# A graph-attention layer and a graph-convolution layer on one core: the last chunk's parts for Wo moved forward, and the residuals' biases added by accumulating transfers

## The chip, the cores and the metric

The kernel runs on one core of a Trainium2 chip. The metric is the device time of one execution in microseconds. Before the change it is 2554.0 us, the median of 3 runs (2552.22 to 2556.43).

## What is computed

The input `x` has 64 samples of 256 rows by 512 columns in float32; `adj` is a 256 by 256 matrix of zeros and ones. Two layers follow one another, each ending in a residual sum and a layer norm.

```python
# layer 0: attention over 8 heads of 64, masked by adj
q, k, v = x @ Wq + bq, x @ Wk + bk, x @ Wv + bv
attn = softmax(q k^T / 8 + (1 - adj) * -1e9)
x = layernorm(x + (attn @ v) @ Wo + bo)
# layer 1: graph convolution
x = layernorm(x + (adj @ x) @ weight + bias)
```

## The kernel before

The samples are worked off in 32 pairs (512 rows). Software pipelining turns each pair's work into a "window": in window `w` the kernel does the attention of pair `w`, the projections v, q, k of pair `w + 1`, and the second layer and the output product of pair `w - 1`. A window repeats 30 times; a different sequence opens and another closes the run.

The products with the five weights are made in three parts to keep float32 accuracy on a faster multiplication: every left factor is cut into `high`, `low` and `diff`, and so is every weight. VectorE makes the cuts. For the second factor of Wo (called `o`) and of the second layer's weight (`l`) the left factor is cut in four chunks of 128 rows:

```python
    def cut_low(a, cut, low):
        nc.vector.tensor_scalar(cut.bitcast(I32), a.bitcast(I32), -int(FINE), None, op0=OP.bitwise_and)
        nc.vector.tensor_tensor(low, a, cut, op=OP.subtract)
    # [...]
    def chunk_parts(name, p, j):          # one chunk: three VectorE instructions
        a = (O if name == "o" else Y)[p, j // 2][:, j % 2].rearrange("p k i -> p (k i)")
        cut = one.tile([P, D], F32, name="cut")
        high, low = (chunks.tile([P, D], F32R, name=n) for n in ("chigh", "clow"))
        diff = differences.tile([P, D], F32R, name="cdiff")
        cut_low(a, cut, low)
        difference(a, low, diff)
        # [...]
        later(1, chunk_high, name, p, j)  # ScalarE copies the high part one step later
    # [...]
    def near(name, p, j):                 # TensorE: low part first, then high
        chunk_high(name, p, j)
        pm = BANKS[name, p, j] = ps_mm.tile([P, D], F32, name="mm")
        if (name, p, 1) in WP:
            part_product(pm, name, p, j, 1)
        part_product(pm, name, p, j, 0)
        # [...]
    def far(name, p, j):                  # TensorE: the diff part, later
        # [...]
```

`later(n, f)` puts a step off by `n` ticks; a tick passes after each block of products. In the windows the orders of TensorE, ScalarE and VectorE are those in which the program names the steps. GpSimd's order is chosen by the scheduler.

The three parts of each weight lie in device memory and are loaded again for every window, in tiles of 1 MB, through a ring of six tiles, by GpSimd's DMA queue:

```python
    def load_w(n=1):
        # [...] the order is o, v, q, k, l in each window, three parts each
                t = wring.tile([P, DC, D], F32R, name="wr")
                nc.gpsimd.dma_start(t, SCRATCH[name, i])
```

The residual `R` of a pair is loaded by SyncE's queue into one of two buffers, 1 MB each, as soon as the pair that held the buffer has been stored. The biases are added to it by VectorE, one instruction of 128 x 1024 for each sample and layer:

```python
    def load_r(p):
        t = rpool.tile([P, 2, NC, D], F32, name="r")
        nc.sync.dma_start(t, xr[p])
    # [...]
    def biased(p, b, bias):
        nc.vector.tensor_tensor(R[p][b], R[p][b], bias[:, None, :].to_broadcast([P, NC, D]), op=OP.add)

    def with_bo(p, b):
        biased(p, b, bo_s)
```

`bo_s` holds `bo` plus the product of `bv` and Wo, on all partitions; `b1_s` the second layer's bias. The bias of the second layer is added when `R`'s rows have been read for `adj @ x` (`later(1, biased, p, b, b1_s)` in `adj_x`).

The attention's exponentials of a unit lie in two tiles, `e0` and `e1`. VectorE multiplies each by the mask (`masked`), then sums both (`summed`) for the denominators. The order of a window is put together here:

```python
            later(1 + kc, masked, p, u, kc)
    # [...]
        seq = slot + co[2:3] + o[:1] + f1 + co[3:] + o[1:2] + PENDING[:6] + o[2:] + PENDING[6:] + slot + v + q[:1] + slot + q[1:] + f1 + \
            y[:1] + f0 + y[1:2] + k[:1] + (cl[:1] if w < NP - 2 else []) + y[2:] + f0 + bo_steps + slot + k[1:2] + \
            (cl[1:2] if w < NP - 2 else [])
```

`slot` is an attention unit, `co`/`cl` are the cuts of the chunks of Wo and of the second layer, `o`, `v`, `q`, `k`, `l` the blocks of products, `y` the products with `adj`, `f1`/`f0` the `far` parts that are still owed (all but one, or all), `PENDING` the cuts of the next input.

Of the kernel before, what the change touches and what calls it, by code (L numbers as in the profile page):

```python
# [20 lines left out]
F32 = mybir.dt.float32  # L21
# [3 lines left out]
OP = mybir.AluOpType  # L25
AX = mybir.AxisListType

P = 128
# [9 lines left out]
def tile_adj_resnorm(tc, x, adj, wq, bq, wk, bk, wv, bv, wo, bo, w1, b1, out):  # L38
    good = fast(tc, x, adj, wq, bq, wk, bk, wv, bv, wo, bo, w1, b1, out)
    with tc.If(good < P):  # L40
        general(tc, x, adj, wq, bq, wk, bk, wv, bv, wo, bo, w1, b1, out)


def fast(tc, x, adj, wq, bq, wk, bk, wv, bv, wo, bo, w1, b1, out):

    nc = tc.nc
    B, N, D = x.shape
    HD = D // H
    DC = D // P
    NC = N // P  # L50
    NP = B // 2
# [19 lines left out]
    scratch = pool("scratch", 1, space=bass.MemoryType.DRAM)  # L71
# [8 lines left out]
    XC, R, XF, XG, XL, XD, Q, K, V, E, SM, O, HL, Y, ST, CP, CUT = ({} for _ in range(17))  # L80
# [27 lines left out]
    def on_all(b, name):  # L108
        t = cpool.tile([P, D], F32, name=name)
        nc.sync.dma_start(t, b.partition_broadcast(P))  # L110
        return t
# [18 lines left out]
    def raw_weight(name, tiles, queue):  # L130

        for i in range(3):
            SCRATCH[name, i] = scratch.tile([P, DC, D], F32, name=f"{name}{i}")
        n = DC // len(tiles)
        for i, t in enumerate(tiles):
            for k in range(n):
                RAW[name, i * n + k] = t[:, k]
            w = SOURCE[name][i * n * P:(i + 1) * n * P]
            if name == "o":


                for a in range(n):
                    queue.dma_start(t[:, a], w.rearrange("(h a i) e -> a h i e", h=4, a=2)[a])
            else:
                queue.dma_start(t, w.rearrange("(c p) e -> p c e", p=P))
# [44 lines left out]
    bo_s, b1_s = on_all(bo, "bo"), on_all(b1, "b1")  # L190
# [7 lines left out]
    def adj_t():  # L198
# [10 lines left out]
        nc.vector.tensor_reduce(acc[:, 0:1], square, AX.XY, OP.max)  # L209
        nc.vector.tensor_scalar(acc, acc, RANGE * RANGE, None, op0=OP.mult)  # L210

    def bv_wo():

        wide = one.tile([P, DC, P], F32, name="vc")
        nc.vector.tensor_copy(wide, bv_s[:, :, None].to_broadcast([P, DC, P]))
        pm = ps_mm.tile([P, D], F32, name="mm")
        for d in range(DC):
            nc.tensor.matmul(pm, wide[:, d, :], RAW["o", d], start=d == 0, stop=d == DC - 1)
        nc.vector.tensor_tensor(bo_s, bo_s, pm, op=OP.add)

# [2 lines left out]
    def later(n, f, *args):  # L225
        due.append([n, f, args])

    def tick():
        for d in due:
            d[0] -= 1  # L230
        ready = [d for d in due if d[0] <= 0]
        due[:] = [d for d in due if d[0] > 0]
        for _, f, args in ready:
            f(*args)
# [124 lines left out]
    def scores(p, u):  # L359
        g, b = UNITS[u]  # L360
        for kc in range(NC):

            sc = [ps_at.tile([P, 2, N], F32, name="at") for s in range(2)]
            for a in range(2):
                for s in range(2):
                    r = slice(s * HD, (s + 1) * HD)
                    nc.tensor.matmul(sc[s][:, a, :], K[p, g][r, a, b, kc * P:(kc + 1) * P], Q[p, g][r, a, b, :],  # L367
                                     start=True, stop=True)
            e = E[p, u, kc] = one.tile([P, 2, 2, N], F32, name=f"e{kc}")
            for s in range(2):  # L370
                nc.scalar.activation(e[:, s], sc[s], AF.Exp, scale=qscale)  # L371
            later(1 + kc, masked, p, u, kc)

    def masked(p, u, kc):
        e = E[p, u, kc].rearrange("p s a n -> p (s a) n")
# [47 lines left out]
        nc.gpsimd.tensor_tensor(acc, acc, seen, op=OP.add)  # L423


    def biased(p, b, bias):

        nc.vector.tensor_tensor(R[p][b], R[p][b], bias[:, None, :].to_broadcast([P, NC, D]), op=OP.add)

    def with_bo(p, b):  # L430
        biased(p, b, bo_s)

    def norm(p, name):

# [66 lines left out]
    def adj_x(p, i):  # L501
        b, half = divmod(i, 2)
        if half == 0:
            Y[p, b] = four.tile([P, NC, DC, P], F32, name="o")
        while (p, b, half) not in HL:
            tick()
        hl = HL.pop((p, b, half))
        pm = ps_mm.tile([P, 2, N], F32, name="mm")
        for j in range(2):
            for mc in range(NC):  # L510
                for i in range(2):
                    nc.tensor.matmul(pm[:, j, :], hl[:, i, mc, j * P:(j + 1) * P], adjT[:, mc, :],  # L512
                                     start=mc == 0 and i == 0, stop=mc == NC - 1 and i == 1)
        nc.scalar.activation(Y[p, b][:, :, 2 * half:2 * half + 2].rearrange("p c j i -> p j c i"), pm.rearrange("p j (c i) -> p j c i", c=NC), AF.Copy)
        if half:
            later(1, biased, p, b, b1_s)
        if p < NP - 2 and b == 0:
            later(1, halves, p, 1, half)

# [20 lines left out]
    def between(w):  # L540

        ahead, behind = w + 1, w - 1
        b = lambda name: [(block, name, behind if name in "ol" else ahead, j) for j in range(4)]
        v, q, k, o, l = (b(n) for n in "vqkol")
        c = lambda name, p: [(chunk_parts, name, p, j) for j in range(4)]
        y = [(adj_x, behind, i) for i in range(4)]
        bo_steps = [(with_bo, w, b) for b in range(2)]
        x_steps = [(x_t, w + 2, i) for i in range(4) if w + 2 < NP]
        x1 = [[s for f in (x_t, x_parts) for s in [(f, w + 2, i)] if w + 2 < NP] for i in range(4)]
        x2 = [[(x_diff, w + 2, i)] if w + 2 < NP else [] for i in range(4)]  # L550
        slot, f1 = [None], [(caught_up, 1)]
        f0 = [(caught_up,)]
        split = lambda name: [(split_w, name, i) for i in range(4)]
        mixed = lambda m, n: [s for pair in zip(m, n) for s in pair]
        halves_tiles = lambda: [one.tile([P, 2, D], F32, name=f"hl{i}") for i in range(2)]
        if w == -1:
            return [(x_t, 0, i) for i in range(4)] + mixed(v, split("v")) + mixed(q, split("q")) + [(adj_t,)] + \
                mixed(k, x_steps)
        if w == 0:
            raw_weight("o", halves_tiles(), nc.sync)  # L560
            PENDING[:] = [s for m, n in zip(x1, x2) for s in m + n]
            return slot + mixed(v, split("k")) + slot + q[:3] + split("o") + [(bv_wo,), (load_w, 3)] + \
                [(lambda: raw_weight("l", halves_tiles(), nc.sync),)] + slot + q[3:] + k[:2] + split("l") + \
                [(load_r, 0)] + slot + k[2:] + bo_steps + c("o", w)[:2] + \
                [(load_w, 3), (load_r, 1)]
        co, cl = c("o", behind), c("l", behind)
        seq = slot + co[2:3] + o[:1] + f1 + co[3:] + o[1:2] + PENDING[:6] + o[2:] + PENDING[6:] + slot + v + q[:1] + slot + q[1:] + f1 + \
            y[:1] + f0 + y[1:2] + k[:1] + (cl[:1] if w < NP - 2 else []) + y[2:] + f0 + bo_steps + slot + k[1:2] + \
            (cl[1:2] if w < NP - 2 else [])
        PENDING[:] = x1[3] + x2[3]  # L570
        if w == NP - 2:
            co = c("o", w)
            return seq + k[2:3] + co[:1] + k[3:] + co[1:2] + [(block, "o", w, 0)] + cl[:1] + [(block, "o", w, 1)] + cl[1:2]
        seq += k[2:3] + cl[2:3] + k[3:] + x1[0] + l[:1] + f1 + x2[0] + x1[1] + x2[1] + l[1:2] + cl[3:] + \
            l[2:3] + c("o", w)[:1] + x1[2] + x2[2] + l[3:] + f1 + c("o", w)[1:2]
        return seq

    PENDING = []

    def slot(before, unit):  # L580
        if before[0] >= 0:
            values(*before)
        scores(*unit)

    def steps(seq, units):
        for step in seq:
            if step is None:
                before = units.pop(0)
                step = slot, before, units[0]
            f, *args = step  # L590
            f(*args)
            if f in (block, slot, adj_x, values, split_w):
                tick()

    def window(w):
        steps(between(w), [(w - 1, 3)] + [(w, u) for u in range(4)])

    def last_window():
# [15 lines left out]
        def some(what):  # L614


            for word in what.split():
# [6 lines left out]
                else:  # L624
                    yield chunk_parts if word[0] == "c" else block, word[-3], pairs[word[-2]], int(word[-1])

        bo_steps = [(with_bo, q, b) for b in range(2)]
        seq = [None, (rows_of_q,), *some("lr0 cop2 lr1 cop3 op2 clr2 op3 clr3 f slot yp0 lr2 yp1"), *bo_steps,
               *some("slot coq0 lr3 coq1 oq0 clp0 oq1 clp1 f slot lp0 clp2 lp1 clp3 yq0"), (values, q, 3),
# [202 lines left out]
```

## Time and profile before

| what | value |
|---|---|
| time, median of 3 | 2554.0 us |
| span of the profiled execution | 2553.1 us |
| TensorE (PE) busy | 2496.0 us, 98% |
| VectorE (DVE) busy | 1872.6 us, 73% |
| ScalarE (ACT) busy | 1705.7 us, 67% |
| GpSimd (POOL) busy | 382.4 us, 15% |
| moved by DMA | 600.25 MB, mean 235 GB/s |
| of which GpSimd's queue (q0) | 475.03 MB, 51.9% of 16 engines' span |
| of which SyncE's queue (q1) | 121.42 MB, 22.0% of 16 engines' span |

A busy TensorE isn't a TensorE at its peak: the ends of its instructions are modelled and overlap, so what matters is the distance between the starts of neighbouring groups of products. The timeline gives these starts. A group of four products of 128 x 512 starts every 0.91 us where nothing waits. The same step of neighbouring windows starts 77.4 us apart. What VectorE does is only of interest where TensorE waits for it, and the same holds for the transfers.

### The profile page before, as it was taken

Reading aid. Unit: us, or ns where it says so; the run is one execution under the profiler, and the core shown is the slowest. Engines: PE = TensorE matmul, PEld = TensorE weight load, DVE = VectorE, ACT = ScalarE, POOL = GpSimd, SP = SyncE. Lnnn points to the kernel's source line nnn. Section 1 sums busy time; section 2 is a strip of 40 time slices with the busy share of each in tenths; the row PEclk is TensorE's granted clock in tenths of the full one; section 3 lists DMA queues with packets and bytes.
Section 4 is the critical chain, followed back from the end, with each engine's and each line's share of the span. In section 5 each row is a group of like instructions: output and inputs, shape, how many; then the busy total and the mean of one; then the engine's idle time right before and its main releaser. Section 6 shows DMA issues by size and latency. Waiting matters only on the chain.

```text
span 2553.1 us, 42184 instructions
## 1 busy us (share of the span) xinstructions
PE 2496.0 (98%) x15806; PEld 1886.6 (74%) x15806; DVE 1872.6 (73%) x3239; ACT 1705.7 (67%) x3206; POOL 382.4 (15%) x793
## 2 busy tenths in 40 slices
PE   8999999999999999999999999999999999999997
PEld 4477777777777777777777777777777777777765
DVE  4676787677886677876767876768876778866786
ACT  4557666776666766666776667766667766677755
POOL 0111111111111111111111111111111111111101
PEclk9999999999999999999999999999999999999998
DMA  7868778778788687777787787787787787777711
GB/s 205 284 201 273 235 232 259 240 244 243 240 256 247 236 263 232 235 250 252 231 274 226 232 259 243 240 262 234 246 246 247 251 247 233 247 254 229 257 68 51
DMA packets 375744, 600.25 MB, mean 235 GB/s; under 512 B 273520, under 2 KB 273776, under 8 KB 317552
## 3 DMA queue, kind: packets, MB, share of 16 engines
q0 software_dynamic: 65232, 475.03, 51.9%
q1 hardware_dynamic: 309760, 121.42, 22.0%
q8 instruction: 127, 2.08, 0.3%
q10 hardware_dynamic: 544, 1.05, 0.1%
q14 instruction: 81, 0.66, 0.1%
HBM read 548.15 MB, written 49.28 MB: 234 GB/s over the span
## 4 chain that ended last, share of the span: by engine, by line
PE 70%; DVE 25%; issue 3%; DMA 1%; ACT 0%; POOL 0%; SPq 0%; DVEq 0%; ACTq 0%
PE mm L314 50%; PE at L367 7%; PE at L402 6%; PE mm L512 5%; DVE clow L169 4%; DVE r L338 3%; DVE cdiff L174 3%; DVE diff L174 2%; DVE cut L168 2%; PE at L394 2%; DVE e L376 2%; DVE low L169 2%; DVE xT L264 2%; DVE x L168 1%; DVE o L418 1%
## 5 line engine op out<-in xcount | busy, mean ns | idle before, releaser
L326 ACT ACTIVATE mm<-mm 128x512 f32<-128x512 f32 x616 | 357.8, 581 | 356.7 <-PE mm L314 356.6
L376 DVE TENSOR_TENSOR e<-e,adjT 128x1024 f32<-128x1024 f32 x256 | 307.6, 1221 | 34.2 <-ACT e L371 34.2
L314 PE MATMUL mm<-wr,clow 128*128 128x512 f32 x1024 | 285.1, 401 | 25.1 <-DVE clow L169 24.6
L371 ACT ACTIVATE e<-at 128x512 f32<-128x512 f32 x512 | 265.2, 604 | 52.9 <-PE at L367 52.9
L314 PE MATMUL mm<-wr,chigh 128*128 128x512 f32 x1024 | 279.9, 396 | 0.7
L314 PE MATMUL mm<-wr,cdiff 128*128 128x512 f32 x1024 | 269.6, 391 | 5.9 <-ACT mm L326 5.9
L314 PE MATMUL mm<-low,wr 128*128 128x512 f32 x960 | 265.1, 398 | 0.0
L314 PE MATMUL mm<-high,wr 128*128 128x512 f32 x960 | 257.2, 390 | 0.0
L367 PE MATMUL at<-qT,kT 64*128 64x256 f32 x2048 | 256.6, 389 | 0.1
L314 PEld LDWEIGHTS mm<-wr,clow 128*128 128x128 f32 x1024 | 188.7, 190 | 86.6 <-DVE clow L169 38.3
L314 PE MATMUL mm<-diff,wr 128*128 128x512 f32 x960 | 248.5, 391 | 0.0
L402 PE MATMUL at<-e,v 128*32 128x256 f32 x4096 | 246.9, 381 | 0.0
L367 PEld LDWEIGHTS at<-qT,kT 64*128 64x128 f32 x2048 | 190.6, 186 | 67.7 <-issue 53.0
L499 DVE TENSOR_TENSOR hl<-r,hl 128x512 fp32r<-128x512 f32 x122 | 84.3, 691 | 203.4 <-ACT hl L498 203.4
L314 PEld LDWEIGHTS mm<-wr,chigh 128*128 128x128 f32 x1024 | 191.5, 189 | 53.0 <-ACT chigh L298 14.2
L314 PEld LDWEIGHTS mm<-wr,cdiff 128*128 128x128 f32 x1024 | 192.5, 188 | 48.1 <-ACT mm L326 7.8
L444 ACT ACTIVATE z<-r,mean 128x512 bf16<-128x512 f32 x240 | 172.6, 719 | 76.2 <-DVE mean L436 71.2
L314 PEld LDWEIGHTS mm<-low,wr 128*128 128x128 f32 x960 | 173.6, 188 | 51.6 <-issue 19.9
L338 DVE SCALAR_TENSOR_TENSOR r<-mm,r 128x512 f32<-128x512 f32 x240 | 160.4, 687 | 69.6 <-PE mm L314 69.6
L314 PEld LDWEIGHTS mm<-high,wr 128*128 128x128 f32 x960 | 180.3, 188 | 38.4
L476 ACT ACTIVATE r<-r,less,rstd 128x512 f32<-128x512 f32 x248 | 200.4, 808 | 6.1 <-DVE less L469 6.1
L314 PEld LDWEIGHTS mm<-diff,wr 128*128 128x128 f32 x960 | 176.3, 188 | 33.6
(123 smaller groups left out, 3985.0 us busy)
## 6 DMA issues: line engine op xcount, KB each, us to landing
wr<-o POOLq DMA_DIRECT2D x93, 1024.0 KB, 6.3
wr<-v POOLq DMA_DIRECT2D x90, 1024.0 KB, 6.4
wr<-q POOLq DMA_DIRECT2D x90, 1024.0 KB, 6.5
wr<-k POOLq DMA_DIRECT2D x90, 1024.0 KB, 7.3
wr<-l POOLq DMA_DIRECT2D x90, 1024.0 KB, 7.6
x<-in_x_dram SPq DMA_DIRECT2D x496, 64.0 KB, 6.4
r<-in_x_dram SPq DMA_DIRECT2D x31, 1024.0 KB, 5.3
out_dram<-r SPq DMA_DIRECT2D x60, 512.0 KB, 6.5
```

What stands on the lines that cost most here:

```text
L169: nc.vector.tensor_tensor(low, a, cut, op=OP.subtract)
L174: nc.vector.scalar_tensor_tensor(diff, low.bitcast(F32), -(FINE + 1), a, op0=OP.mult, op1=OP.add)
L314: nc.tensor.matmul(pm, *operands(name, p, j, i, k), start=k == 0 and i == begins, stop=k == DC - 1, skip_group_check=True)
L326: nc.scalar.activation(pm, pm, AF.Copy, scale=1 + 1 / FINE)
L338: nc.vector.scalar_tensor_tensor(r, pm, 1.0, r, op0=OP.mult, op1=OP.add, accum_out=ST[p, name][:, j:j + 1])
L367: nc.tensor.matmul(sc[s][:, a, :], K[p, g][r, a, b, kc * P:(kc + 1) * P], Q[p, g][r, a, b, :], start=True, stop=True)
L371: nc.scalar.activation(e[:, s], sc[s], AF.Exp, scale=qscale)
L376: nc.vector.tensor_tensor(e, e, mask[:, kc:kc + 1, :].to_broadcast([P, 4, N]), op=OP.mult)
L402: nc.tensor.matmul(at[h * 32:(h + 1) * 32, a, :], V[p, b][:, kc, col:col + 32], e[kc][:, h % 2, h // 2, :], start=kc == 0, stop=kc == NC - 1)
L444: nc.scalar.activation(waste, R[p][j // 2][:, j % 2], AF.Square, bias=mean[:, j:j + 1], accum_out=squares[:, j:j + 1])
L476: nc.scalar.activation(r, r, AF.Identity, scale=rstd, bias=less)
L512: nc.tensor.matmul(pm[:, j, :], hl[:, i, mc, j * P:(j + 1) * P], adjT[:, mc, :], start=mc == 0 and i == 0, stop=mc == NC - 1 and i == 1)
```

## The change

There are two ideas. First, the cut of the last of the four Wo chunks is placed directly behind that of the third, ahead of the sums that VectorE makes for the second layer's leftover part, and the mask of `e1` in that stretch is put off by one more tick, so that TensorE finds the chunk ready. The cuts of the next input move by a few places for the same reason. Second, VectorE no longer adds the biases to the residuals. GpSimd's DMA queue does, by transfers that add what they bring to what lies in the tile: the bias row is read from device memory and repeated for 128 partitions and two halves. For `bo` a row of it is first stored to device memory. The second layer's bias stays on VectorE for the last two pairs.

```diff
+    bo_row = scratch.tile([1, D], F32, name="bo_row")
@@ bv_wo
         nc.vector.tensor_tensor(bo_s, bo_s, pm, op=OP.add)
+        nc.sync.dma_start(bo_row, bo_s[0:1])
@@ scores
-            later(1 + kc, masked, p, u, kc)
+            later(1 + kc * (1 + (u == 0 and 1 < p < NP - 1)), masked, p, u, kc)
@@
-    def biased(p, b, bias):
-        nc.vector.tensor_tensor(R[p][b], R[p][b], bias[:, None, :].to_broadcast([P, NC, D]), op=OP.add)
+    def biased(p, b, row):
+        nc.gpsimd.dma_start(R[p][b], row[:, None, :].to_broadcast([P, NC, D]), accum_op=OP.add)
     def with_bo(p, b):
-        biased(p, b, bo_s)
+        biased(p, b, bo_row[0:1].to_broadcast([P, D]))
+    def with_b1(p, b):
+        if p < NP - 2:
+            biased(p, b, b1.partition_broadcast(P))
+        else:
+            nc.vector.tensor_tensor(R[p][b], R[p][b], b1_s[:, None, :].to_broadcast([P, NC, D]), op=OP.add)
@@ adj_x
-            later(1, biased, p, b, b1_s)
+            later(1, with_b1, p, b)
@@ between
-        seq = slot + co[2:3] + o[:1] + f1 + co[3:] + o[1:2] + PENDING[:6] + o[2:] + PENDING[6:] + slot + v + [...]
+        x_now = (PENDING[:6], [], PENDING[6:]) if w == 1 else ([], PENDING[:], [])
+        seq = slot + co[2:3] + o[:1] + co[3:] + f1 + o[1:2] + x_now[0] + o[2:3] + x_now[1] + o[3:] + x_now[2] + slot + v + [...]
```

More of the change, by code (lines that the diff above doesn't have):

```diff
@@ L565, in between @@
                 [(load_w, 3), (load_r, 1)]
+        x_now = (PENDING[:6], [], PENDING[6:]) if w == 1 else ([], PENDING[:], [])
         co, cl = c("o", behind), c("l", behind)
-        seq = slot + co[2:3] + o[:1] + f1 + co[3:] + o[1:2] + PENDING[:6] + o[2:] + PENDING[6:] + slot + v + q[:1] + slot + q[1:] + f1 + \
+        seq = slot + co[2:3] + o[:1] + co[3:] + f1 + o[1:2] + x_now[0] + o[2:3] + x_now[1] + o[3:] + x_now[2] + slot + v + q[:1] + slot + q[1:] + f1 + \
             y[:1] + f0 + y[1:2] + k[:1] + (cl[:1] if w < NP - 2 else []) + y[2:] + f0 + bo_steps + slot + k[1:2] + \
```

## The prediction

> **What bounds the kernel.** I read the page's busy table first, then TensorE's waits, then the timeline of one window, then the groups by shape and the stages.
>
> ```profile
> PE 2496.0 (98%) x15806; PEld 1886.6 (74%) x15806; DVE 1872.6 (73%) x3239; ACT 1705.7 (67%) x3206; POOL 382.4 (15%) x793
> PE mm L314 <- DVE clow L169: 24.6, 33, 2.2
> PEld mm L314 <- DVE clow L169: 38.3, 33, 2.6
> PEld mm L314 <- ACT chigh L298: 14.2, 31, 0.5
> ```
>
> TensorE is the bound, with 57 us of 2553.1 idle in all. The largest single wait (24.6 us in 33 places; the columns are total, times, longest) is for `clow`, the low part of a chunk. The timeline of TensorE in one window shows where it sits:
>
> ```profile
> 1217.69 1.07 PE L314 MATMUL mm<-wr,clow 128*128 128x512 f32 x4
> 1218.60 1.07 PE L314 MATMUL mm<-wr,chigh 128*128 128x512 f32 x4
> 1219.50 1.07 PE L314 MATMUL mm<-wr,cdiff 128*128 128x512 f32 x4
> 1221.18 1.21 PE L314 MATMUL mm<-wr,clow 128*128 128x512 f32 x4 [0.60 <-DVE clow L169]
> 1222.40 1.20 PE L314 MATMUL mm<-wr,chigh 128*128 128x512 f32 x4
> 1223.44 1.08 PE L314 MATMUL mm<-wr,cdiff 128*128 128x512 f32 x4
> 1224.45 0.64 PE L394 MATMUL at<-sm,ones 128*32 128x256 f32 x8
> ```
>
> The first column is the start. Groups follow at 0.91 us, but from 1219.50 to 1221.18 there are 1.68: the fourth Wo chunk comes 0.77 late. The next three starts are 1.22, 1.04 and 1.01 apart, another 0.55 lost while the weight loads and the high part catch up. So 1.32 us per window are lost here, of which about 0.09 are the ordinary step to the attention's products. Measured over all starts, the same 1.30 to 1.32 stands in each of 29 windows (38 us). Elsewhere in a window starts depart from their usual spacing by little, chiefly where the product's shape changes.
>
> Why VectorE is late: from 1258 to 1229 of the next window it works almost without a gap. Its queue in the stretch:
>
> ```profile
> 1216.25 0.42 DVE L168 TENSOR_SCALAR cut<-o 128x512 int32<-128x512 int32 x1
> 1216.70 0.69 DVE L169 TENSOR_TENSOR clow<-o,cut 128x512 fp32r<-128x512 f32 x1
> 1217.43 0.69 DVE L174 SCALAR_TENSOR_TENSOR cdiff<-clow,o 128x512 fp32r<-128x512 f32 x1
> 1218.04 1.22 DVE L376 TENSOR_TENSOR e<-e,adjT 128x1024 f32<-128x1024 f32 x1
> 1219.17 0.68 DVE L338 SCALAR_TENSOR_TENSOR r<-mm,r 128x512 f32<-128x512 f32 x1
> ...
> 1219.98 0.42 DVE L168 TENSOR_SCALAR cut<-o 128x512 int32<-128x512 int32 x1
> 1220.43 0.69 DVE L169 TENSOR_TENSOR clow<-o,cut 128x512 fp32r<-128x512 f32 x1
> ```
>
> Between the third chunk's cut and the fourth's (1218.04 to 1219.98) stand the mask of `e1`, a residual sum and its mean. The biases lie 40 us earlier in the same gapless stretch:
>
> ```profile
> L428 DVE TENSOR_TENSOR r<-r,b 128x1024 f32<-128x1024 f32 x62 | 75.6, 1219 | 0.0
> L428 DVE TENSOR_TENSOR r<-r,bo 128x1024 f32<-128x1024 f32 x62 | 73.0, 1219 | 2.4 <-DMA r<-in_x_dram 2.4
> ```
>
> [...]
>
> **Part 1, the order.** TensorE's own order stays the same. The fourth cut moves from 1219.98 to 1218.04, 1.94 us earlier, so `clow` is ready at about 1219.2 where TensorE wants it at 1220.41. The stall should go with 1.2 us to spare. The mask and the sum of `e` behind it slip by the cut's 1.8 us; `sm` would be ready at about 1223.1 to 1223.6, and TensorE now wants it at 1223.2. Alone that leaves up to 0.4.
>
> **Part 2, VectorE without biases.** 124 of the 128 additions go but for the four of the last two pairs' second layer: 75.6 + 73.0 + 4.8 us of 128 instructions, less 4 x 1.2 = 149 us of VectorE's 1872.6. Per window 4 instructions at a spacing of 1.14 = 4.6 us. In the stretch above, VectorE is then ahead by some 2 to 4 us (until it meets inputs that aren't there yet), which also covers the `sm` of part 1. TensorE gains nothing beyond the waits: 29 x (1.32 - 0.09) = **35.7 us**. Window 0 adds some. There VectorE waits 2.41 us for `R`'s first load, does two biases (2.36) and is then the cause of TensorE's waits of 2.25 and 1.94 for `clow` at 122.9 and 127.0. About **5 us** of that should go. The tail gains under 1. Sum of the gains: 41 us, so about 2513 if nothing new waits.
>
> **Part 3, what the transfers cost.** Each moves 512 KB into `R`; four per window. GpSimd's order by the scheduler puts them so: the first `bo` ahead of the third k tile, the second ahead of the three l tiles, both second-layer biases behind these and ahead of the o tiles. The queue's landing times in the trace let me set up the slack of each weight. The third k tile is issued at 1250.04 in this window (863.2, 1095.3 in others), lands 5.7 to 8.3 us later (median 7.2) and is first used 12.5 after its issue: slack 4.2 to 7.4, median 5.2, the smallest of v, q and k (6.5 and more for the others). The stages around it:
>
> ```profile
> 1083.80:1093.50 9.70, 9.70 (x81) 6.96 (x80) 3.29 (x8) 7.89 (x17) 2.31 (x5) 1.00 0.97 342
> 1093.50:1103.20 9.70, 9.70 (x49) 8.10 (x47) 3.71 (x5) 8.06 (x14) 1.67 (x3) 1.00 0.86 318
> 1103.20:1112.90 9.70, 9.70 (x93) 7.54 (x91) 8.66 (x13) 6.73 (x14) 0.92 (x3) 1.00 0.62 224
> 1112.90:1122.60 9.70, 9.70 (x45) 7.92 (x43) 9.19 (x13) 5.66 (x11) 1.10 (x2) 1.00 0.33 108
> ```
>
> The last two columns are the DMA engines' share and GB/s: nearly full just there, light some 15 us later.
>
> `R`'s load is issued 1.8 us before to 1.2 after that k tile (0.6 before on average) and needs some 4.1 alone (its packets take 3.7 to 4.0 of data when uncrossed). So `bo` starts some 3.6 us after the k tile's old issue, and the k tile 0.7 behind. How long is 512 KB of one repeated row? At the start the two biases are read so, 128 packets of 2 KB each. The packet records show these 256 packets in 3.4 us, 200 to 500 ns for many, where distinct rows take 84 ns each. So I take 3.4 us for an accumulate, about 150 GB/s, not the 1.4 of a plain load. The k tile then has its data behind `bo`'s: 3.6 + 1.2 + 3.4 + 3.2 (a tile's data, from pairs of loads landing 3.2 apart) + 0.4 = 11.8 of the 12.3 to 12.5 it has. With a spread of 1 us in `R`'s landing, a wait of about 0.4 per window remains: **12 us**. The rest of the queue is then l, two biases and o: l still lands before its use, o's second tile about 1 us ahead. I add 5 us for late ones.
>
> Sum: 2554.0 - 41 + 12 + 5 = **2530**.
>
> **Rivals.**
> 1. *The k tile or the o tiles wait for the accumulates.* For it: the queue is in order, the DMA engines are at 0.86 to 0.97 in the stage, the repeated row is slow, and whether adding slows a packet further no run shows. With 4.5 us each, 4 x 1.1 more per window pile up, k waits 0.9 and the o tiles up to 3: up to 28 x 3.9 = 109 us lost for 41 gained, so up to 2620. Against it: the DMA share falls to 0.62 and 0.33 in the next two stages, where the queue can recover.
> 2. *The transfers are free* (the repeated row runs at full rate): 2508 to 2515.
> 3. *VectorE was not the wait that counts.* Had TensorE another wait just behind, `sm` or ScalarE's high part, only 0.5 of the 1.32 would go: about 2540. For it: the 14.2 us of weight loads waiting for `chigh`. Against it: ScalarE's copy follows the cut by a tick and moves with it.
>
> **Range and chances.** The gain is bounded by 41 us, so under 2502.9 (over 2% faster) would need more than the waits hold: 0.04. Over 2605 needs rival 1 in full: 0.09. The range reaches from the full gain, 2508, to 2590, long upwards because the length of an accumulate is the least known number.
>
> **What would show it.** Right: the `clow` wait in TensorE's list falls from 24.6 us in 33 places to under 5; the timeline has 0.91 from the third diff group to the fourth low group; VectorE's busy time falls by about 149 us; the window's period goes from 77.4 to about 76.5. Wrong: TensorE waits with a DMA of `wr` as releaser, in the far part of the first k block or in the o blocks; accumulates landing more than 6 us after issue; a DMA share near 1 over the 20 us from the k tile on.

## The result, and the profile after

The changed kernel takes **2657.2 us** (median of 4 runs, 2654.3 to 2664.2) against 2555.2 for the kernel before in the same comparison: a ratio of 1.0405, 95% interval 1.038 to 1.043. It is 4% slower. Predicted were 2530 with a range of 2508 to 2590. Both kernels have the same order of instructions on TensorE, so every microsecond is a wait or a slower clock. The page's busy table and TensorE's list of waits (total, times, longest) of the kernel after:

```profile
PE 2525.3 (95%) x15806; PEld 1906.8 (72%) x15806; DVE 1739.3 (66%) x3115; ACT 1710.2 (64%) x3206; POOL 540.8 (20%) x917
```

```profile
PE mm L317 <- DMA wr<-k: 73.9, 29, 4.3
PE mm L317 <- DMA wr<-q: 7.9, 1, 7.9
...
PE mm L317 <- DMA wr<-l: 3.5, 1, 3.5
...
PE mm L317 <- DVE clow L169: 2.7, 3, 1.9
```

VectorE's busy time fell by 133 us and the wait for `clow` from 24.6 us to 2.7. In its place TensorE waits for a k tile in 29 places. The timeline of TensorE shows one of them:

```profile
1222.88 1.07 PE L317 MATMUL mm<-high,wr 128*128 128x512 f32 x4
1223.78 2.05 PE L522 MATMUL mm<-adjT,hl 128*128 128x256 f32 x16
1229.35 1.74 PE L317 MATMUL mm<-diff,wr 128*128 128x512 f32 x4 [3.52 <-DMA wr<-k]
1231.03 1.08 PE L398 MATMUL at<-sm,ones 128*32 128x256 f32 x8
1231.88 2.51 PE L406 MATMUL at<-e,v 128*32 128x256 f32 x32
```

The diff part of the first k block should start at about 1225.7 and starts at 1229.35. Then the groups are stretched (1.74 us for four products in place of 1.07). The table by stages shows why; its columns are the stretch, its length, the busy time and number of PE, PEld, DVE, ACT and POOL, the granted clock, the DMA share and GB/s:

```profile
1225.80:1229.40 3.60, 0.08 (x2) 0.08 (x1) 0.13 (x1) 0.73 (x2) 0.66 (x1) 1.00 1.08 282
1229.40:1232.80 3.40, 3.40 (x24) 1.70 (x28) 0.14 (x1) 1.07 (x2) 0.00 (x0) 0.54 1.10 410
```

After the wait TensorE's granted clock is 0.54 over 3.4 us. The timeline of GpSimd shows who stood ahead of the k tile, in this window and, in the last line, at the same place of the next:

```profile
1218.44 1.27 POOL L432 DMA_DIRECT2D r<-bo_row  x1 [10.45 <-ACT mm L329]
1219.26 1.06 POOL L127 DMA_DIRECT2D wr<-k  x1
1219.82 1.70 POOL L432 DMA_DIRECT2D r<-bo_row  x1
1220.56 2.63 POOL L127 DMA_DIRECT2D wr<-l  x3
...
1300.76 1.27 POOL L432 DMA_DIRECT2D r<-bo_row  x1 [10.64 <-DMA r<-in_x_dram]
```

In the next window the view names what the accumulate waited for, the landing of `R`'s load. In the first it names ScalarE, but there too SyncE issued `R`'s load at 1212.42, 6.0 us ahead of `bo`. The DMA issues (number, KB each, median us from issue to landing) show that the queue is slow from there on; before, the k tiles took 7.3 us and the l tiles 7.6:

```profile
wr<-k POOLq DMA_DIRECT2D x90, 1024.0 KB, 8.4
wr<-l POOLq DMA_DIRECT2D x90, 1024.0 KB, 15.5
...
r<-in_x_dram SPq DMA_DIRECT2D x31, 1024.0 KB, 5.4
r<-bo_row POOLq DMA_DIRECT2D x62, 512.0 KB, 9.9
```

Where the 99.4 us between the two spans lie, from the starts of the v block in each window (0.5 of them lie behind TensorE's end):

| stretch | after less before, us |
|---|---|
| up to the first v block | -2.5 |
| window 0 (the q tile's wait, 7.9) | +8.0 |
| the 28 windows behind it | +87.6 |
| from the last v block to TensorE's end (a k tile's wait, 2.6, and an l tile's, 3.5) | +5.8 |

In the 28 windows the diff part of the first k block starts 76 us late in sum (71 by the list of waits, which counts from the modelled end of the group before). There are 14 spells of half clock (granted 0.50), 54.6 us long with 2.3 in which TensorE was still waiting; half of the rest is lost, 26. The fourth Wo chunk gives back 0.56 per window or 16. Together that is 86 of the 87.6.

### The profile page after: what moved, and what is told of

The parts are those of the page before. It is cut to its first block, busy times and chain, and to the rows that moved or that the text cites. A ratio compares the mean times of both kernels' runs of the same rounds, so it can differ in the third digit from the quotient of the medians.

```text
span 2652.5 us, 42543 instructions
## 1 busy us (share of the span) xinstructions
PE 2525.3 (95%) x15806; PEld 1906.8 (72%) x15806; DVE 1739.3 (66%) x3115; ACT 1710.2 (64%) x3206; POOL 540.8 (20%) x917
## 4 chain that ended last, share of the span: by engine, by line
PE 41%; DMA 28%; DVE 15%; ACT 8%; issue 6%; POOL 1%; SPq 1%; DVEq 0%; POOLq 0%; ACTq 0%
PE mm L317 29%; DMA wr<-k 10%; DMA out_dram<-r 8%; DMA r<-in_x_dram 6%; PE at L406 5%; PE at L370 5%; ACT z L454 4%; DMA x<-in_x_dram 3%; DVE clow L169 3%; DVE r L341 3%; PE at L398 2%; DVE cdiff L174 2%; ACT r L486 2%; DVE cut L168 1%; ACT v L350 1%
## 5 line engine op out<-in xcount | busy, mean ns | idle before, releaser
L317 PE MATMUL mm<-diff,wr 128*128 128x512 f32 x960 | 256.9, 400 | 73.9 <-DMA wr<-k 73.9
L406 PE MATMUL at<-e,v 128*32 128x256 f32 x4096 | 261.8, 397 | 0.0
L317 PEld LDWEIGHTS mm<-wr,clow 128*128 128x128 f32 x1024 | 187.8, 189 | 71.9 <-DVE r L341 16.5
L406 PEld LDWEIGHTS at<-e,v 128*32 128x32 f32 x4096 | 145.5, 116 | 94.8 <-issue 20.7
L416 DVE STREAM_TRANSPOSE z<-zc 128x256 f32<-128x256 f32 x128 | 56.5, 441 | 226.8 <-ACT zc L400 226.7
```

The source lines that it names most:

```text
L317: nc.tensor.matmul(pm, *operands(name, p, j, i, k), start=k == 0 and i == begins, stop=k == DC - 1, skip_group_check=True)
L406: nc.tensor.matmul(at[h * 32:(h + 1) * 32, a, :], V[p, b][:, kc, col:col + 32], e[kc][:, h % 2, h // 2, :], start=kc == 0, stop=kc == NC - 1)
L416: nc.vector.transpose(z, zc)
```

## Experiments

The theory from the trace: GpSimd issues its transfers one after the other, and they land in that order (all 577 in the trace of after, all 453 in that of before), so the accumulate's wait for `R`, and then its packets, delay the weights issued behind it. Rivals: the wait for `R` alone is enough; the size of the accumulate alone; and, for the missing gain, that VectorE had never been what held up the fourth chunk. All ratios are against the kernel before on the same chip.

**e1: GpSimd in program order.** The program names the accumulates behind the k and l tiles; only the scheduler had put them ahead.

```diff
-    with tc.manual_schedule(engines={PE, Activation, DVE}):
+    with tc.manual_schedule(engines={PE, Activation, DVE, Pool}):
```

> The changed kernel with one edit: in the windows GpSimd also keeps the order of the program, so both bo accumulates stand behind the third k tile, the three l tiles and the b1 accumulates. The transfers are the same 122 by size and source. Theory (place in the queue): the third k tile no longer waits for R's load and for bo's data, the 73.9 us of TensorE waiting for wr<-k go to under 3, the half-clock spells behind these waits go too, and the time is 2520 to 2545. Rival (volume: the added 62 MB fill the DMA engines, whatever the order): TensorE waits for another weight instead and the time stays above 2600.

Measured: 2539.2 us, ratio 0.9949 (0.9933 to 0.9966). No wait for a k tile is left, with the same bytes moved and the same accumulates. So all of the 118 us between after (2657.2) and here hang on the place in the queue. GpSimd's timeline now has the biases last:

```profile
1238.90 0.61 POOL L127 DMA_DIRECT2D wr<-k  x1 [5.16 <-PE mm L317]
1242.53 0.53 POOL L127 DMA_DIRECT2D wr<-l  x1 [3.02 <-PE mm L317]
...
1251.05 2.73 POOL L432 DMA_DIRECT2D r<-bo_row  x2
```

**e2: the order of steps alone**, all biases on VectorE as before.

```diff
-        biased(p, b, bo_row[0:1].to_broadcast([P, D]))
+        nc.vector.tensor_tensor(R[p][b], R[p][b], bo_s[:, None, :].to_broadcast([P, NC, D]), op=OP.add)
-        if p < NP - 2:      # with_b1: never by transfer
+        if False:
```

> The changed order of the steps alone, all biases on VectorE as before. As predicted in part 1, the 1.32 us per window at the fourth Wo chunk would mostly go: 2520 to 2530. Theory from the trace after: the residual sum that frees a PSUM bank now stands behind the fourth cut, so the wait for clow turns into a wait for that bank and for sm, and with VectorE no less loaded than before only 0 to 0.6 us per window come back: 2537 to 2557.

Measured: 2538.7, ratio 0.9946 (0.993 to 0.9963), the same as e1 although VectorE has 124 additions more. The median period of a window is 76.82 us in both (77.38 before), and in the window compared TensorE's groups start at the same places to within 0.03 us.

**e6: the transfers alone**, steps in the order of before, GpSimd in program order.

```diff
-            later(1 + kc * (1 + (u == 0 and 1 < p < NP - 1)), masked, p, u, kc)
+            later(1 + kc, masked, p, u, kc)
-        seq = slot + co[2:3] + o[:1] + co[3:] + f1 + o[1:2] + x_now[0] + [...]
+        seq = slot + co[2:3] + o[:1] + f1 + co[3:] + o[1:2] + PENDING[:6] + [...]
```

> The steps in the order of the kernel before, all biases by accumulating transfers, and GpSimd's steps in the order in which the program names them, so that no k tile stands behind one. Theory A (what VectorE is spared is given back as waits for ScalarE at the attention unit, before the Wo chunks): the fourth chunk is as late as before, 2545 to 2556 us. Theory B (part 2 of the prediction, VectorE ahead by 2 to 4 us at the Wo chunks): the stall of 1.3 us a window goes, 2518 to 2530.

Measured: 2556.5, ratio 1.0011 (1.0005 to 1.0018). The wait for the chunk is still there, in TensorE's list:

```profile
PE mm L317 <- DVE clow L169: 20.2, 31, 1.9
```

VectorE is busy for 132 us less (1740.1 against 1872.6), and this is worth nothing here: the median period is 77.35. VectorE's timeline of before shows the place where three of a window's additions stood:

```profile
1262.87 1.22 DVE L428 TENSOR_TENSOR r<-r,b 128x1024 f32<-128x1024 f32 x1
1264.01 2.35 DVE L428 TENSOR_TENSOR r<-r,bo 128x1024 f32<-128x1024 f32 x2
1266.28 0.44 DVE L412 STREAM_TRANSPOSE z<-zc 128x256 f32<-128x256 f32 x1
...
1267.54 0.69 DVE L418 TENSOR_TENSOR o<-vc,zc 128x512 f32<-128x512 f32 x1
1268.15 2.36 DVE L376 TENSOR_TENSOR e<-e,adjT 128x1024 f32<-128x1024 f32 x2
```

and that of e1 what stands there without them:

```profile
1250.98 0.69 DVE L174 SCALAR_TENSOR_TENSOR cdiff<-clow,o 128x512 fp32r<-128x512 f32 x1
1253.64 0.45 DVE L416 STREAM_TRANSPOSE z<-zc 128x256 f32<-128x256 f32 x1 [1.97 <-ACT zc L400]
...
1255.51 0.69 DVE L422 TENSOR_TENSOR o<-vc,zc 128x512 f32<-128x512 f32 x1 [0.71 <-ACT vc L409]
1257.03 2.36 DVE L380 TENSOR_TENSOR e<-e,adjT 128x1024 f32<-128x1024 f32 x2 [0.82 <-ACT e L374]
```

1.97, 0.71 and 0.82 us of idle time stand there, 3.5 together, and the three additions in the kernel before took 1.14 + 2.27 = 3.4. VectorE only arrives earlier at values that ScalarE hasn't made yet. Behind these waits VectorE of e6 is 0.35 us ahead of before, counted from the v block's start in one window, and at the Wo chunks 0.05.

**e3: a small `bo`.** The accumulate covers 128 partitions x 32 elements (the rest of `bo` is left out): 128 packets of 128 bytes per transfer in place of 256 of 2 KB.

```diff
+        nc.gpsimd.dma_start(R[p][b][:, 0:1, 0:32], bo_row[0:1, 0:32].to_broadcast([P, 32])[:, None, :], accum_op=OP.add)
```

> The changed kernel with each bo accumulate cut to 128 x 32 elements (16 KB in place of 512 KB); the rest of the bias bo is left out. Its place at the head of GpSimd's queue and its wait for R's load stay. Theory that wait and transfer are both needed: the k tile is issued about 5 us later than before the change but has no data ahead of it, lands 10.5 us after its old issue against 12.5 it has: TensorE waits under 0.5 us per window, 2525 to 2550. Rival (the wait for R's load alone is enough): 1.5 us and more per window remain, 2590 and above.

Measured: 2611.8, ratio 1.0238 (1.0219 to 1.0257), far over the theory's 2550 and in the rival's range (e5 speaks against the rival). With 3% of the bytes more than half of the loss remains. TensorE's list and GpSimd's timeline:

```profile
PE mm L317 <- DMA wr<-k: 49.7, 28, 3.8
```

```profile
1196.93 1.82 POOL L435 DMA_DIRECT2D r<-bo_row  x2 [10.69 <-DMA r<-in_x_dram]
1198.13 1.18 POOL L127 DMA_DIRECT2D wr<-k  x1
```

The edit also changed the scheduler's order: in all 28 windows both accumulates now stand ahead of the third k tile, where in after only the first does. So again 256 packets are ahead of it. Each takes only 35 ns, but the first 128 are spread over 1.5 us and the next 128 over 3.1, together as long as the 4.6 us of the 256 packets of 2 KB in after. So the bytes alone aren't what holds up the queue. This left two candidates, the wait and the number of packets.

**e5: `bo` on 16 partitions x 32 elements**, 16 packets per transfer (the rest of `bo` is left out). The wait for `R` stays, and as in e3 both accumulates stand ahead of the third k tile.

```diff
+        nc.gpsimd.dma_start(R[p][b][0:16, 0:1, 0:32], bo_row[0:1, 0:32].to_broadcast([16, 32])[:, None, :], accum_op=OP.add)
```

> The kernel after, GpSimd's order by the scheduler as there, but bo is added to 16 partitions x 32 elements of each half-residual only (16 packets per transfer in place of 256; the rest of bo is left out). It keeps the wait of GpSimd's queue for R's load and takes the packets away. Theory A (both the wait at the queue's head and the number of accumulating packets are needed to make TensorE wait): the third k tile is issued some 6.7 us ahead of its use, needs 5.3 to land, so it waits for it less than 0.5 us a window; 2535 to 2550 us. Theory B (the wait for R's load at the queue's head is enough by itself): TensorE waits for the k tile over 1 us a window as before; 2590 or more.

Measured: 2540.8, ratio 0.9953 (0.9937 to 0.997). TensorE's list:

```profile
PE mm L317 <- DMA wr<-k: 7.2, 8, 1.6
```

The k tile is issued 6.2 us ahead of its use in e3 and in e5 alike (medians), but lands 1.9 us after it in e3 and 0.3 ahead of it here, and what differs is the accumulates' packets ahead of it, 256 and 32. The wait for `R` alone uses up the k tile's slack and exceeds it only in some windows; on top of it the packets cost TensorE. That the wait is needed too has no run of its own: none puts the packets ahead of the k tile without it. The trace of after speaks for it. Over its 29 windows TensorE is the later, the later `bo` is issued (correlation 0.90): 1.5 us late where `bo` is issued 8.5 ahead of the tile's use, 4.5 where it is 6.5. A straight line through them (an estimate) reaches zero at 9.4, and the tile's old issue stood 12.5 ahead.

**e12: distinct rows.** `bo` is stored on 128 rows, and the accumulate reads these.

```diff
-    bo_row = scratch.tile([1, D], F32, name="bo_row")
+    bo_row = scratch.tile([P, D], F32, name="bo_row")
-        nc.sync.dma_start(bo_row, bo_s[0:1])
+        nc.sync.dma_start(bo_row, bo_s)
-        biased(p, b, bo_row[0:1].to_broadcast([P, D]))
+        biased(p, b, bo_row)
```

> The kernel after, but bo is stored to device memory on all 128 rows and each accumulate reads these distinct rows (each twice) in place of one row 256 times. Theory A (the adding makes the packets slow): packets as in after, some 177 ns and more, wait for the k tile as in after, 2645 to 2670 us. Theory B (the repeated row makes them slow): packets near 84 ns, bo's data in some 2 us in place of 4.2, wait for the k tile under 1.2 us a window, 2560 to 2610.

Measured: 2617.2 in 2 runs, ratio 1.0246 (1.0201 to 1.0291); neither figure was met. The accumulating packets have a median of 178 ns as in after, so the repeated row isn't what makes them slow. Nor does it look like the queue: the plain 8 KB packets of the weights, on the same queue, have a median of 325 ns, 81 for each 2 KB. What is left is the adding (an inference: no run has plain 2 KB packets on that queue). But the first `bo` needs 3.2 us for its 256 packets in place of 4.6: in after they come in at up to 46 per half microsecond, drop to 17 and rise to 28 again (medians), and that dip is absent here. So the one repeated row has a share in that dip. It isn't the whole of it, as the biases in e1 are repeated rows too, and there the 256 packets of each take 2.5 to 3.5 us (medians of the four in a window). The k tile gains only 0.7 us per window (its waits are 54.3 us against 73.9), and its own packets are slower then (a mean of 0.44 us for 8 KB against 0.34 in after). What runs beside them there was not tried.

**e4: `bo` by VectorE, the second layer's bias by transfers.**

```diff
-        biased(p, b, bo_row[0:1].to_broadcast([P, D]))
+        nc.vector.tensor_tensor(R[p][b], R[p][b], bo_s[:, None, :].to_broadcast([P, NC, D]), op=OP.add)
```

> The changed kernel with bo added by VectorE again and only the second layer's bias by accumulating transfers (60 of 512 KB, behind the l tiles). Theory (place in the queue): no wait for wr<-k, 2525 to 2545. Rival (accumulating transfers as such hurt, in proportion to their number): about half of the loss stays, near 2605.

Measured: 2541.6, ratio 0.9956 (0.9939 to 0.9972). No wait for k. So the loss of the changed kernel hangs on `bo` alone; the other bias is issued behind the l tiles and harms nothing in the windows (median period 76.80).

**e7: other work into the idle places.** If the spared time is lost because VectorE waits for ScalarE, cuts that are ready should be put there. Two cuts of the second layer move up, on e1; `bo` of the last pair is added by VectorE.

```diff
-            [...] + f0 + bo_steps + slot + k[1:2] + (cl[1:2] if w < NP - 2 else [])
+            [...] + f0 + bo_steps + (cl[1:2] if w < NP - 2 else []) + slot + k[1:2]
-        seq += [...] + l[:1] + f1 + x2[0] + x1[1] + x2[1] + l[1:2] + cl[3:] + [...]
+        seq += [...] + l[:1] + cl[3:] + f1 + x2[0] + x1[1] + x2[1] + l[1:2] + [...]
```

> The changed order, GpSimd in program order, biases by transfers (bo of the last pair by VectorE), and two cuts of the second layer's chunks placed ahead of the places where VectorE waits for ScalarE or for TensorE, so that the time freed is used there. Theory A (the freed time is lost in those waits, and can be used by moving other work into them): VectorE is some 1.8 us ahead in the gapless stretch, the remaining 0.76 us a window at the fourth Wo chunk goes, 2514 to 2524 us. Theory B (what remains at the fourth chunk has another cause): as without the moves, 2535 to 2541.

Measured: 2543.8, ratio 0.9963 (0.9951 to 0.9976). My expectation failed: the median period is 76.83, as without the moves. VectorE's timeline shows how:

```profile
1270.43 0.69 DVE L174 SCALAR_TENSOR_TENSOR diff<-low,xT 128x512 fp32r<-128x512 f32 x1
1272.75 0.69 DVE L341 SCALAR_TENSOR_TENSOR r<-mm,r 128x512 f32<-128x512 f32 x1 [1.64 <-PE mm L317]
```

It did come 1.6 us ahead, and then waited 1.64 us for TensorE at a residual sum 22.8 us ahead of the next v block. Only the next idle place had been found.

**e8: the same moves, biases on VectorE.** Its moves are those of e7, on e2.

> The same order of steps as the run with the moved cuts, but all biases added by VectorE. Theory A (the stretch ahead of the attention unit is full with the four biases in it, so moving more work there gains nothing): 2534 to 2550 us, no gain over the changed order alone (2538.7). Theory B (the moves pay by themselves, and the transfers are of no use): 2514 to 2524.

Measured: 2538.5, ratio 0.9946 (0.9929 to 0.9962): no gain over e2. With the additions in place VectorE waits 0.23 us at that sum.

**e9: that place filled as well**, on e7. The first Wo chunk's cut moves ahead of the sum; all but the last two pairs' second-layer biases are transfers.

```diff
-        seq += [...] + x2[1] + l[1:2] + l[2:3] + c("o", w)[:1] + x1[2] + [...]
+        seq += [...] + x2[1] + c("o", w)[:1] + l[1:2] + l[2:3] + x1[2] + [...]
```

> As the run with the moved cuts and the biases by transfers, where VectorE came 1.6 us ahead and then lost it waiting for TensorE at the residual sum 22.8 us before the window's v block. Here the cut of the first Wo chunk (1.87 us) stands ahead of that sum; bo of the last pair is by transfer again. Theory A (the lead is kept if every wait on the way is filled with work that is ready): VectorE reaches the third and fourth Wo chunks some 1.4 us earlier, the sum that frees the fourth chunk's PSUM bank and the sum of e come in time, the remaining 0.76 us a window goes; period 76.1, 2516 to 2526 us. Theory B (what remains at the fourth chunk is not VectorE's lateness): period 76.8, 2536 to 2542.

Measured: **2519.8**, ratio 0.9865 (0.9848 to 0.9881), as expected by the first theory; the median period is 76.13. Counted from the v block before, VectorE reaches the residual sums among the Wo chunks 1.0 us earlier than in e7. TensorE's timeline at the Wo chunks (the fourth chunk is the third `clow`):

```profile
1274.21 1.07 PE L317 MATMUL mm<-wr,clow 128*128 128x512 f32 x4
...
1276.03 1.07 PE L317 MATMUL mm<-wr,clow 128*128 128x512 f32 x4
1276.93 1.07 PE L317 MATMUL mm<-wr,chigh 128*128 128x512 f32 x4
1277.84 1.07 PE L317 MATMUL mm<-wr,cdiff 128*128 128x512 f32 x4
1278.75 1.07 PE L317 MATMUL mm<-wr,clow 128*128 128x512 f32 x4
1279.65 1.07 PE L317 MATMUL mm<-wr,chigh 128*128 128x512 f32 x4
```

All starts are 0.9 apart: the whole 1.23 us per window of the prediction is gained.

**e10: the residual sum ahead of the fourth cut**, on e9.

```diff
-        seq = slot + co[2:3] + o[:1] + co[3:] + f1 + o[1:2] + [...]
+        seq = slot + co[2:3] + o[:1] + f1 + co[3:] + o[1:2] + [...]
```

> The same, and the residual sum that frees the fourth chunk's PSUM bank stands ahead of the fourth chunk's cut, as in the kernel before (the mask stays put off). Theory A: with VectorE ahead either order is in time, within 3 us of the other. Theory B (the bank is still late there): up to 9 us faster than the other order.

Measured: 2518.8, ratio 0.9856 (0.9839 to 0.9872); no difference to e9. Once VectorE is ahead, either order is in time. Which order is better while VectorE isn't ahead, with the mask put off, was not run.

**e11: the moves of e9 with all biases on VectorE.**

> The moved cuts, the first Wo chunk's cut ahead of the sum, all biases on VectorE. In the run with the moved cuts on VectorE the wait at that sum was only 0.2 us. Theory A (VectorE has no time left with the biases on it): gains at most 0.2 us a window, 2532 to 2540 us. Theory B (the order alone does it): 2516 to 2526.

Measured: 2531.3, ratio 0.9909 (0.9893 to 0.9926). It gains 0.75 us per window at the fourth chunk, 0.19 more than e2, as expected of a VectorE with 0.2 us to spare. So the transfers are worth 11 to 12 us (e9 against e11, which differ in GpSimd's order too), but only with the order that uses them.

## Why the prediction was wrong, step by step

The mechanism that made it slower is its rival 1 in the k tile's form, with 2657 beyond even that rival's 2620. Of the 127 us between 2530 and 2657 some 65 are the k tile's lateness beyond the 12 foreseen, 28 the clock and 20 the gain missing at the fourth chunk; the rest is late tiles, window 0 and what isn't traced. Rival 1 had the mechanism, but for 4.5 us per accumulate, close to the 4.6 measured, it foresaw 0.9 us of wait for k and up to 3 for the o tiles. Measured are 2.55 for k and none for o. The signs that it named came: the releaser is a `wr` DMA at the first k block, the `bo` accumulates land 9.9 us after their issue (its limit was 6), and the DMA share is 0.98 to 1.10 around the wait.

- **Part 1, the order: the step "The stall should go with 1.2 us to spare" failed.** `clow` of the fourth chunk did come in time. VectorE's and TensorE's timelines of after, in one window:

```profile
1264.37 0.69 DVE L169 TENSOR_TENSOR clow<-o,cut 128x512 fp32r<-128x512 f32 x1
1265.17 0.69 DVE L174 SCALAR_TENSOR_TENSOR cdiff<-clow,o 128x512 fp32r<-128x512 f32 x1
1265.78 0.68 DVE L341 SCALAR_TENSOR_TENSOR r<-mm,r 128x512 f32<-128x512 f32 x1
```

```profile
1265.31 1.07 PE L317 MATMUL mm<-wr,cdiff 128*128 128x512 f32 x4
1266.52 1.20 PE L317 MATMUL mm<-wr,clow 128*128 128x512 f32 x4
1267.56 1.08 PE L317 MATMUL mm<-wr,chigh 128*128 128x512 f32 x4
```

`clow` ends at 1265.06, TensorE wants it at 1266.22 and starts at 1266.52. The product needs one of four PSUM tiles, and the residual sum that frees it now stands behind the cut: it starts at 1265.78 and the product 0.74 later. The page's group of weight loads for `clow` names it as the releaser (16.5 us in all):

```profile
L317 PEld LDWEIGHTS mm<-wr,clow 128*128 128x128 f32 x1024 | 187.8, 189 | 71.9 <-DVE r L341 16.5
```

I had counted the mask and `sm` among what slips, not that sum. Also `sm` came 0.21 late, within the 0.4 allowed. Together 0.56 of 1.23 us per window were gained; 29 x 0.56 = 16, and e2 measured 15. The share of the sum is read from this releaser and these times, not from a run of its own. Rival 3 foresaw another wait right behind, and its 2540 is what e1 and e2 show. But that number is in part luck: it named `sm` or the high part and held that VectorE was not the wait that counts, and the sum and `sm` are VectorE's.

- **Part 2: the step "VectorE is then ahead by some 2 to 4 us" failed.** The bracket "(until it meets inputs that aren't there yet)" was the whole matter. It meets them at once (e1's timeline), and again 15 us later (e7's). The 149 us were 133 of busy time (durations of 1.22 us stand 1.14 apart, so part of each overlaps its neighbour, which is most of the difference) and worth 0 as time (e6). With the idle places filled the 35.7 us of the sum do exist: e9 gains 34.2. The 5 us in window 0 were 2.5 at the first v block's start; the other runs with transfers for `bo` have 0.0 (e9) to 4.6 (e5) there, so this part isn't explained.

- **Part 3: the step "= 11.8 of the 12.3 to 12.5 it has" failed, and it cost most.** The sum was right in its form, and three of its four terms were too small. Counted from the k tile's old issue, as medians over the windows:

| term | predicted | measured |
|---|---|---|
| issue of `bo` | 3.6 | 5.1 |
| to its first packet | 1.2 | 2.0 |
| its data | 3.4 | 4.6 |
| the tile's data and landing | 3.6 | 3.2 |
| sum, against the 12.5 available | 11.8 | 14.9 |

The excess, 2.4, fits the measured wait (mean 2.55). Most of the largest error, 1.5 us, was to be read: I took 4.1 us for `R`'s load from packet times where nothing crossed them, and the page before has 5.3 from issue to landing in its DMA issues:

```profile
r<-in_x_dram SPq DMA_DIRECT2D x31, 1024.0 KB, 5.3
```

That `bo` waits for this landing was a premise of the author; in after a further 0.5 passes between the landing and `bo`'s issue. The data of an accumulate was an estimate from plain reads; 178 ns for an adding packet is what e12 measured from distinct rows too.

- **Not in the prediction at all: the clock.** The four stages that it shows have a granted clock of 1.00. In after the clock stands at 0.50 for 3.4 us, or 6.8 at the most, at 15 of the 29 waits for k, and the two shortest of these 15 lasted 1.9 us. By the same reckoning as above the spells cost some 28 us with the last window's, over a third of the waits themselves.

- **The 5 us for late tiles** were 11.4: a q tile once (7.9) and an l tile once (3.5), none of them the o tile I had named. (A v tile was 1.9 late at the first v block, which is within the 2.5 above.) With GpSimd in program order the q wait is gone and one l wait of 3.4 stays.

## What to carry to other kernels

Before work is taken off an engine, follow its queue from that place to the wait that counts and look for each input that isn't there: the time spared reaches only as far as the next such wait, unless ready work is moved into it (132 us of VectorE's busy time were worth nothing in e6, and with the idle places filled e9 gained 34.2). Where a transfer that must wait joins a queue that lands in order, as GpSimd's did here, look at what stands behind it and put it where the others have slack; the same transfers cost 118 us ahead of the k tile and nothing measurable behind the l tiles (e1 against e2). For the length of a transfer take issue to landing from the page, in the stage where it will run, not its packets' time alone.

## What the runs showed of the hardware

- An accumulating packet of 2 KB from GpSimd's queue takes 178 ns (median in after and in e12), against 84 for a plain read of a distinct row of that size on SyncE's queue (`R`'s load in before) and 325 for a plain packet of 8 KB on GpSimd's (before and after); 256 of them, 512 KB, take 2.5 us at best (e1), and 4.6 where one repeated row was read in the full stage (after, DMA share 0.98 to 1.10), 3.2 there with distinct rows (e12).
- Packets of 128 bytes that add take 35 ns each, but 256 of them were spread over 4.7 us ahead of the k tile (e3), as long as the 256 of 2 KB there (after). They left 49.7 us of waits for k, and 32 such packets in that place 7.2 (e5).
- In after TensorE's clock was halved at all 8 waits for k of 3.0 us or more, at 5 of 10 between 2.0 and 3.0, and at 2 of 11 below (1.26 to 1.90). The shortest wait with a spell lasted 1.9 us, the longest without one 2.9.
